# A megakernel's first part ordered anew: durations of the steps as the trace has them, and the standard deviation as a step of its own

## The chip, the cores and the metric

The kernel runs on one core of a Trainium2 chip. The metric is the device time of one execution in microseconds. Before the change it is 3328.47 us, the median of 3 runs (3323.04 to 3329.41).

## The reference

Sixteen images and texts go through a tokenizer and two layers, each with an attention and a feed-forward stage, all with a width of D = 256 and float32. The changed code lies in the tokenizer, the window attention and the routing of the experts:

```
h = tokens(x)                                  # conv 2x2, softmax(Q K^T / 16) V, 441 rows
h = concat([h, txt], axis=1)                   # 569 rows for each image
h = h + window_attention(layernorm(h))         # shifted windows of 64 rows, 8 heads
h = h + experts(layernorm(h))                  # 8 experts, the best two of each row
h = h + phase_attention(layernorm(h))
h = h + lstm(layernorm(h))

def _layernorm(x, axis=-1, eps=1e-5):
    m = jnp.mean(x, axis=axis, keepdims=True)
    v = jnp.var(x, axis=axis, keepdims=True)
    return (x - m) / jnp.sqrt(v + eps)
```

## The kernel before, in words

The rows of two images make a pair p (0 to 7), and a pair is cut into nine chunks c of 128 rows, each two windows of 64. Everything up to the scatter of the rows to their experts is the first part (about 950 of 3332 us). Behind it lie the experts, the phase attention and the recurrent network.

The first part's instructions are written out by a planner that runs while the kernel is built. Each stream of work is a Python generator. It yields the engine and the duration of its next step ("PE", 0.25), then issues the instruction. `Order.run` holds, for each engine, the time at which it would be free. It takes, of all streams, the step that could start first (ties go to the lower rank, then to the older stream), adds its duration and goes on. So the order of the instructions on TensorE, VectorE, ScalarE and GpSimd is fixed at build time by these durations, and the chip's waits come on top. A duration has no other effect. "DVE+" and "POOL+" mark steps that are not laid side by side with each other. `first.fork` starts a new stream that goes on beside the one that forks it.

The streams are: `features` (the convolution), `projections` (`tq`, `tv`), two of `tokens` (scores `tsc` in line 611, transposes `tpt`, averages `tav` in line 639, the rows `h`), `norms` (statistics and normalized rows `wxn`), four of `windows`, `routing` (softmax over the experts, ranks, positions `at`) and, forked, `sent_rows` (the second norm) and `send` (for each chunk two scatters by an indirect DMA in line 927). A chunk's window work on TensorE goes: transposes `wtr` (line 724), queries and keys `wqk` (734), scores `wsc` (752), values `wv` (768) and gate (777), transposes of the probabilities `wpt` (807), averages `wav` (819), output `wob` (830). Between them lie copies on ScalarE and VectorE: `wxT` (728), the keys `KB` (708, on both engines), queries `wq` (743), scaled scores `wS` (758), maximum (782), values `VB` (790), subtraction on GpSimd (794), exponential (796), sum and normalization (799 to 803), `wPT` (812), `wAT` (826).

`norm` (lines 657 to 674) takes VectorE's statistics, then does on GpSimd in one step: variance plus epsilon (668), to the power -1/2 (669), and, for the window's norm, to the power 1/2 (671). That last one, the standard deviation, is kept in a spare column of the row tile and read by line 784, which scales the gate's logits. Then VectorE normalizes (673). The pair of mean and variance has one buffer for all windows.

SP, which issues most DMAs (stores `HD`, loads of the experts' rows `xs` and weights `w`, of the recurrent weights `W_hh` and `W_ih`), isn't under the planner. The framework orders it by its own rules.

Of the kernel before, what the change touches and what calls it, by code (L numbers as in the profile page):

```python
# [10 lines left out]
F32 = mybir.dt.float32  # L11
BF16 = mybir.dt.bfloat16
AF = mybir.ActivationFunctionType
ALU = mybir.AluOpType
# [3 lines left out]
D = 256  # L18
# [3 lines left out]
E = 8  # L22
# [275 lines left out]
def kernel(ctx: ExitStack, tc: tile.TileContext, a: dict, out: bass.AP):  # L298
    nc = tc.nc
# [33 lines left out]
    def place_of(name, slot):  # L333
        return ps.tile([128, 512], F32, name=name, tag=f"first{slot}", bufs=1)
# [18 lines left out]
    slot = route.tile([128, NP, 2, NC], F32, name="slot")  # L353
# [24 lines left out]
    first = Order()  # L378
# [13 lines left out]
    def rows_of(p, c):  # L392

        while len(made) >= ROWS:
            before = ("normed", *made[len(made) - ROWS])
            if before in first.events:
                break
            yield "at", before
        made.append((p, c))
        H[p, c] = hp.tile([128, D + E + 1], F32, name=f"h{p}_{c}", tag="h", bufs=ROWS)  # L400
        return H[p, c]
# [198 lines left out]
    def tokens(slot):  # L600

        last = NIMG - 384
        for n in range(slot, 7 * NP, 2):
            p, c = divmod(n, 7)
            for s in range(2):
                yield "at", ("values", 2 * p + s)
            sc = place_of(f"tsc{n}", 4 + slot)
            for m in range(2):
                yield "PE", 0.76, "64"
                for s in range(2):  # L610
                    nc.tensor.matmul(
                        sc[64 * s : 64 * s + 64, :NIMG], QT[s][:, m, 64 * c : 64 * c + 64],
                        fTs[2 * p + s][:, m, :], start=(m == 0), stop=(m == 1),
                    )
            top = wk.tile([128, 1], F32, name=f"ttop{n}", tag=f"ttop{slot}", bufs=1)
            yield "DVE", 0.61
            nc.vector.tensor_reduce(top, sc[:, :NIMG], AX.X, ALU.max, negate=True)
            P = wk.tile([128, NIMG], F32, name=f"tP{n}", tag=f"tP{slot}", bufs=1)
            share_ = wk.tile([128, 1], F32, name=f"tsum{n}", tag=f"tsum{slot}", bufs=1)
            yield "ACT", 0.85  # L620
            nc.scalar.activation(P, sc[:, :NIMG], AF.Exp, bias=top, accum_out=share_)
            pt = place_of(f"tpt{n}", 4 + slot).rearrange("p (t n) -> p t n", t=4)
            for t in range(4):
                m = min(128, NIMG - 128 * t)
                yield "PE", TURN
                nc.tensor.transpose(pt[:m, t, :], P[:, 128 * t : 128 * t + m], ident)
            yield "DVE", 0.17
            nc.vector.reciprocal(share_, share_)
            PT = wk.tile([128, 4, 128], F32, name=f"tPT{n}", tag=f"tPT{slot}", bufs=1)
            yield "ACT", 0.5  # L630
            nc.scalar.copy(PT[:, :3, :], pt[:, :3, :])
            yield "ACT", 0.28
            nc.scalar.copy(PT[:last, 3, :], pt[:last, 3, :])
            mm = place_of(f"tav{n}", 4 + slot)[:, :D]
            for t in range(4):
                m = min(128, NIMG - 128 * t)
                yield "PE", 0.44, "64"
                for s in range(2):
                    nc.tensor.matmul(
                        mm[64 * s : 64 * s + 64, :], PT[:m, t, 64 * s : 64 * s + 64],  # L640
                        TV[s][:m, t, :], start=(t == 0), stop=(t == 3),
                    )
            if c < 6:
                yield from rows_of(p, c)
                to = [(slice(0, 128), c)]
            else:
                yield "at", ("text", p)
                to = [(slice(lo + 64 * s, hi + 64 * s), i) for s in range(2)
                      for lo, hi, i in ((0, 25, 6), (32, 64, 8))]
            for q, i in to:  # L650
                yield "DVE", 0.48
                nc.vector.scalar_tensor_tensor(
                    H[p, i][q, :D], mm[q], share_[q], tok_b[q], ALU.mult, ALU.add
                )
            first.mark(("token", p, c))

    def norm(h, to, name, slot):

        st = wk.tile([128, 6], F32, name=f"{name}_st", tag=f"st{slot}", bufs=1)
        yield "DVE", 0.43  # L660
        nc.vector.bn_stats(st, h[:, :D])
        mv = wk.tile([128, 2], F32, name=f"{name}_mv", tag=f"mv{slot}", bufs=1)
        yield "DVE", 0.18
        nc.vector.bn_aggr(mv, st)
        rstd = wk.tile([128, 1], F32, name=f"{name}_rstd", tag=f"rstd{slot}", bufs=1)
        yield "POOL", 0.85 if name[0] == "r" else 1.28
        over = mv[:, 1:2]
        nc.gpsimd.tensor_scalar(over, over, EPS, None, ALU.add)
        nc.gpsimd.tensor_tensor(rstd, over, mhalf[:, :1], ALU.pow)
        if name[0] == "w":  # L670
            nc.gpsimd.tensor_tensor(h[:, D + E :], over, half, ALU.pow)
        yield "DVE+", 0.5
        nc.vector.tensor_scalar(to, h[:, :D], mv[:, 0:1], rstd, ALU.subtract, ALU.mult)
        return rstd

    def norms():

        for n in range(NC * NP):
            p, c = unit(n)
            if n >= XNS:  # L680
                yield "at", ("turned", *unit(n - XNS))
            yield "at", ("token", p, min(c, 6)) if c != 7 else ("text", p)
            xn = xns[p, c] = wk.tile([128, D], F32, name=f"wxn{p}_{c}", tag="wxn", bufs=XNS)
            yield from norm(H[p, c], xn, f"w{p}_{c}", "w")
            first.mark(("columns", p, c))

    def sent_rows(p, c, h, slot):

        if p not in XN:
            if p > 1:  # L690
                yield "at", ("sent", p - 2)
            if p not in XN:
                LG[p] = wk.tile([128, NC, E], F32, name=f"LG{p}", tag="LG", bufs=2)
                XN[p] = xnp.tile([128, NC, WIDE], F32, name=f"XN{p}", tag="XN", bufs=2)
                yield "POOL", 0.2
                nc.gpsimd.tensor_copy(XN[p][:, :, D], cols[:, COL["row"] + NC * p : COL["row"] + NC * (p + 1)])
        rstd = yield from norm(h, XN[p][:, c, :D], f"r{p}_{c}", slot)
        yield "DVE", 0.19
        nc.vector.scalar_tensor_tensor(
            LG[p][:, c, :], h[:, D : D + E], rstd, frow("gate_b", E), ALU.mult, ALU.add  # L700
        )
        first.mark(("normed", p, c))

    def half_of_keys(u, kb, qk, rows, engine):
        for r in rows:
            own = slice(32 * r, 32 * r + 32)
            yield engine, 0.4
            (nc.scalar.copy if engine == "ACT" else nc.vector.tensor_copy)(
                kb[own, :, :, r, :], qk[own, 1].rearrange("p m (w x) -> p m w x", w=2)
            )  # L710
        first.mark(("keys", u, engine))

    def windows(slot):

        kb, vb = KB[slot], VB[slot]
        for n in range(slot, NC * NP, WINDOWS):
# [3 lines left out]
            h, xn = H[p, c], xns.pop((p, c))  # L720
# [9 lines left out]
            for m in range(2):  # L730
                for j in range(2):
                    for k in range(2):
                        yield "PE", 0.25
                        nc.tensor.matmul(  # L734
                            qk[:, j, m, :], wqkv[:, k, D * j + 128 * m : D * j + 128 * m + 128],
                            xT[:, k, :], start=(k == 0), stop=(k == 1),
                        )
# [33 lines left out]
                            start=(k == 0), stop=(k == 1),  # L771
                        )
            for k in range(2):
                yield "PE", 0.06, "64"
                for w in range(2):
                    own = slice(64 * w, 64 * w + 64)
                    nc.tensor.matmul(
                        vg[own, D : D + E], xT[:, k, own], gw[:, k, :], start=(k == 0), stop=(k == 1)
                    )
            top = wk.tile([128, NH], F32, name=f"wtop{u}", tag=f"wtop{slot}", bufs=1)  # L780
            yield "DVE", 0.68
            nc.vector.tensor_reduce(top, S, AX.X, ALU.max)
            yield "DVE", 0.2
            nc.vector.scalar_tensor_tensor(
                h[:, D : D + E], vg[:, D : D + E], h[:, D + E :], win_b[:, D:], ALU.mult, ALU.add
            )
            for odd in range(2):
                own = slice(64 * odd, 64 * odd + 64)
                yield "ACT", 0.4
                nc.scalar.copy(  # L790
                    vb[own, :, :, odd, :], v[own].rearrange("p w (g d) -> p w g d", g=4)
                )
# [144 lines left out]
    with tc.manual_schedule(engines=ENGINES):  # L937
# [9 lines left out]
        half = hp.tile([128, 1], F32, name="half")  # L947
# [9 lines left out]
        wk = first_part.enter_context(tc.tile_pool(name="first", bufs=1))  # L957
# [1012 lines left out]
    with tc.manual_schedule(engines=ENGINES):  # L1970
# [5 lines left out]
        wk = bg.enter_context(tc.tile_pool(name="pha", bufs=1))  # L1976
# [170 lines left out]
```

## Time and profile before

| | us |
|---|---|
| median of three runs | 3328.47 |
| profiled execution | 3333.89 |
| its span | 3332.1 |
| TensorE busy in the span | 3026.1 (91%) |
| VectorE / ScalarE / GpSimd busy | 2057.1 / 1448.2 / 821.3 |
| first part: last scatter's end | 954.2 |
| first matmul of the experts | 970.19 |

A profile shows one execution. Busy time is that of an engine's own instructions; the granted clock is the share of full speed that TensorE was allowed. A wait is idle time of an engine before an instruction, put down to what ended it. For an order that is fixed beforehand the waits of the bounding engine, TensorE, are what matters, stretch by stretch.

### The profile page before, as it was taken

What the parts mean: (1) busy time and instruction counts of PE and PEld (TensorE: products, weight loads), DVE (VectorE), ACT (ScalarE), POOL (GpSimd) and SP (SyncE); (2) the same over time, 40 slices, a digit from 0 to 9 for tenths busy, and PEclk for the clock granted to TensorE, in tenths of its full rate; (3) what the DMA queues carried; (4) which work ended last, traced back from release to release, by engine and by line L of the source; (5) the groups of instructions that cost most, each with busy time, mean ns of one, the idle gap of its engine ahead of it and who ended that gap; (6) DMA issues with size and microseconds to landing.
All of it is one profiled execution on the core that took longest, in us unless ns stands there. A gap on an engine that the chain in (4) does not pass through costs nothing.

```text
span 3332.1 us, 134813 instructions
## 1 busy us (share of the span) xinstructions
PE 3026.1 (91%) x57670; PEld 2213.9 (66%) x57670; DVE 2057.1 (62%) x6956; ACT 1448.2 (43%) x4986; POOL 821.3 (25%) x1581
## 2 busy tenths in 40 slices
PE   6999998999859999997999999999999999999884
PEld 3666666666648888885566666766666666666652
DVE  4777777776742322222676777767777777776555
ACT  3544544454312222222454555555555555454442
POOL 1354465445533322222311011011001011000000
PEclk9999999999969999998999999999999999999997
DMA  5111222101167676763334333332333232333333
GB/s 177 57 66 54 71 84 68 46 31 45 41 225 255 237 255 236 251 243 117 114 83 98 86 89 85 78 98 77 95 77 94 78 92 75 86 89 75 93 99 114
DMA packets 275481, 369.73 MB, mean 111 GB/s; under 512 B 144496, under 2 KB 219296, under 8 KB 262208
## 3 DMA queue, kind: packets, MB, share of 16 engines
q1 hardware_dynamic: 249104, 304.71, 30.6%
q0 software_dynamic: 14160, 38.83, 3.1%
q10 hardware_dynamic: 11616, 17.56, 1.8%
q8 instruction: 452, 7.41, 0.9%
q14 instruction: 149, 1.22, 0.1%
HBM read 243.13 MB, written 117.84 MB: 108 GB/s over the span
## 4 chain that ended last, share of the span: by engine, by line
PE 38%; DVE 7%; ACT 5%; issue 2%; DMA 1%; SPq 1%; POOL 0%; ACTq 0%; DVEq 0%; POOLq 0%
PE gates L1811 13%; PE xm_False L1105 5%; PE out_gate L1820 2%; PE z L1105 2%; PE ek L1105 2%; PE v L1105 2%; PE po_False L1105 2%; PE ds_False L1105 2%; PE eq L1105 1%; PE r_False L1105 1%; ACT act L1832 1%; ACT th L1868 1%; DVE ab L1847 1%; DVE cT L1860 1%; DVE act L1853 1%
## 5 line engine op out<-in xcount | busy, mean ns | idle before, releaser
L1811 PEld LDWEIGHTS gates<-W_hh,X 128*16 128x16 f32 (+1 forms) x18176 | 373.2, 103 | 260.3 <-DVE X L1875 246.3
L1811 PE MATMUL gates<-W_hh,X 128*16 128x96 f32 (+1 forms) x18176 | 487.8, 248 | 63.7 <-DVE X L1875 60.9
L1832 ACT ACTIVATE act<-gates 128x96 f32<-128x96 f32 x568 | 142.1, 250 | 446.0 <-PE gates L1811 438.5
L1316 ACT ACTIVATE hT<-hp,w 128x256 f32<-128x256 f32 (+1 forms) x332 | 132.9, 453 | 450.2 <-PE hp L1309 343.4
L1105 PE MATMUL xm_False<-W_ih,dxT_False 128*32 128x256 f32 x4352 | 291.8, 380 | 2.7 <-DVE dxT_False L1341 1.9
L1847 DVE SCALAR_TENSOR_TENSOR ab<-act 128x64 f32<-128x64 f32 x568 | 128.1, 226 | 258.3 <-ACT act L1832 250.8
L1323 PE MATMUL y<-w,hT 128*128 128x256 f32 x1208 | 276.3, 381 | 6.9 <-ACT hT L1316 6.5
L1309 PE MATMUL hp<-xt,w 128*128 128x256 f32 (+1 forms) x1328 | 277.7, 362 | 0.0
L1329 DVE TENSOR_TENSOR ys<-y,w 128x512 f32<-128x512 f32 (+1 forms) x83 | 53.4, 643 | 360.6 <-PE y L1323 315.8
L1754 PEld LDWEIGHTS <-nil 128*32 128x32 bf16 x4552 | 189.5, 94 | 112.7 <-issue 53.7
L1309 PEld LDWEIGHTS hp<-xt,w 128*128 128x128 f32 x1328 | 234.8, 192 | 29.3
L1323 PEld LDWEIGHTS y<-w,hT 128*128 128x128 f32 x1208 | 226.3, 190 | 41.7 <-ACT hT L1316 11.2
L1250 POOL DMA_INDIRECT YT<-ys,to x151 | 147.7, 978 | 416.4 <-DVE ys L1329 389.3
L1820 PE MATMUL out_gate<-W_hh,X 128*32 128x64 f32 x9088 | 232.5, 220 | 1.6 <-issue 1.6
L1760 ACT COPY gates<-xc 128x96 f32<-128x96 f32 x569 | 138.6, 244 | 182.6 <-DMA xc<-XCD 75.5
L1820 PEld LDWEIGHTS out_gate<-W_hh,X 128*32 128x32 f32 x9088 | 186.6, 110 | 4.5 <-issue 1.8
L1875 DVE SCALAR_TENSOR_TENSOR X<-toT,th 128x32 f32<-128x32 f32 x569 | 110.0, 193 | 122.0 <-ACT th L1868 117.4
L1371 POOL TENSOR_SCALAR d_False_rstd<-d_False_mv 128x2 f32<-128x2 f32 (+1 forms) x36 | 9.2, 256 | 673.2 <-DVE d_False_mv L1363 514.9
L1868 ACT ACTIVATE th<-cT 128x32 f32<-128x32 f32 x569 | 130.5, 229 | 94.2 <-DVE cT L1860 43.0
L927 POOL DMA_INDIRECT XS<-XN,at x144 | 149.9, 1041 | 51.6 <-issue 24.9
L734 PE MATMUL wqk<-wxT,wqkv 128*128 128x128 f32 x1152 | 150.9, 280 | 9.6 <-ACT wxT L728 9.2
L734 PEld LDWEIGHTS wqk<-wxT,wqkv 128*128 128x128 f32 x1152 | 140.5, 193 | 25.7 <-ACT wxT L728 16.0
(384 smaller groups left out, 6556.1 us busy)
## 6 DMA issues: line engine op xcount, KB each, us to landing
w<-in_wpack SPq DMA_DIRECT2D x83, 1154.0 KB
taps<-in_taps SPq DMA_DIRECT2D x16, 1764.0 KB
xc<-XCD SPq DMA_DIRECT2D x71, 384.0 KB
XCD<-xp_False SPq DMA_DIRECT2D x256, 96.0 KB
yg<-YT SPq DMA_DIRECT2D x72, 256.0 KB
xs<-XS SPq DMA_DIRECT2D x68, 258.0 KB
HD<-h SPq DMA_DIRECT2D x72, 128.0 KB
fh<-HD SPq DMA_DIRECT2D x72, 128.0 KB
```

The costliest lines, as they stand in the source:

```text
L734: nc.tensor.matmul(qk[:, j, m, :], wqkv[:, k, D * j + 128 * m : D * j + 128 * m + 128], xT[:, k, :], start=(k == 0), stop=(k == 1),)
L927: fill(0, nc.gpsimd.indirect_dma_start(out=XS[0], out_offset=bass.IndirectOffsetOnAxis(ap=at[:, i, c - lo : c - lo + 1], axis=0), in_=XN[p ...
L1105: nc.tensor.matmul(out[own], lhsT[:, own], rhs, start=start, stop=stop)
L1250: keep(nc.gpsimd.indirect_dma_start(out=YT, out_offset=bass.IndirectOffsetOnAxis(ap=to[:, i : i + 1], axis=0), in_=ys[:, i, :], in_offset= ...
L1309: nc.tensor.matmul(hp[:, i, : 128 * n], w1[:, k, hc * 128 : (hc + 1) * 128], xT[:, k, :], start=(k == 0), stop=(k == 1),)
L1323: nc.tensor.matmul(y[:, i, :], hT[:, hc, 128 * i : 128 * i + 128], w2[:, hc, :], start=(hc == 0), stop=(hc == 3),)
L1754: nc.tensor.matmul(g[32 * q : 32 * q + 32, :n], nil[:, :32], nil[:, :n], start=True, stop=last)
L1811: nc.tensor.matmul(GC[32 * q : 32 * q + NB * (1 + half), :96], before[:, kk, NB * (1 - half) :], Whh[:, kk, own : own + 96], start=False, ...
L1820: nc.tensor.matmul(GO[32 * q : 32 * q + 32, :64], before[:, kk, :], Whh[:, kk, own : own + 64], start=False, stop=(kk == 1),)
L1832: nc.scalar.activation(act[:, :96], GC[:, :96], AF.Tanh, scale=0.5), begun.pop((k, t))
L1847: nc.vector.scalar_tensor_tensor(ab, act[:, :64].rearrange("p (g x) -> p g x", g=2), 1.0, act[:, 64:].rearrange("p (g x) -> p g x", g=2), ...
L1868: nc.scalar.activation(th.rearrange("p k x -> p (k x)"), cT, AF.Tanh, scale=0.5)
```

## The change

Eleven durations of the first part get other values: matmul steps (0.76 to 0.745, 0.44 to 0.46, 0.25 to 0.225, 0.06 to 0.087), the normalization on VectorE (0.5 to 0.46), the two small scalings (0.19 to 0.25, 0.2 to 0.22), the key copies (0.4 to 0.46 on ScalarE and 0.53 on VectorE), the value copies (0.4 to 0.47) and GpSimd's step in the norm (0.85 or 1.28 to 0.9). The standard deviation leaves that step: `deviation` is forked as a stream of its own with 0.6 us on GpSimd. Mean and variance of the window's norm get three buffers. What is computed stays the same.

```diff
-                yield "PE", 0.76, "64"
+                yield "PE", 0.745, "64"
...
-                yield "PE", 0.44, "64"
+                yield "PE", 0.46, "64"
...
-        mv = wk.tile([128, 2], F32, name=f"{name}_mv", tag=f"mv{slot}", bufs=1)
+        mv = wk.tile([128, 2], F32, name=f"{name}_mv", tag=f"mv{slot}", bufs=3 if slot == "w" else 1)
...
-        yield "POOL", 0.85 if name[0] == "r" else 1.28
+        yield "POOL", 0.9
...
         if name[0] == "w":
-            nc.gpsimd.tensor_tensor(h[:, D + E :], over, half, ALU.pow)
-        yield "DVE+", 0.5
+            first.fork(deviation(h, over))
+        yield "DVE+", 0.46
         nc.vector.tensor_scalar(to, h[:, :D], mv[:, 0:1], rstd, ALU.subtract, ALU.mult)
         return rstd
+
+    def deviation(h, over):
+        yield "POOL", 0.6
+        nc.gpsimd.tensor_tensor(h[:, D + E :], over, half, ALU.pow)
...
-        yield "DVE", 0.19
+        yield "DVE", 0.25
...
-            yield engine, 0.4
+            yield engine, 0.46 if engine == "ACT" else 0.53
...
-                        yield "PE", 0.25
+                        yield "PE", 0.225
...
-                yield "PE", 0.06, "64"
+                yield "PE", 0.087, "64"
...
-            yield "DVE", 0.2
+            yield "DVE", 0.22
...
-                yield "ACT", 0.4
+                yield "ACT", 0.47
```

## The prediction

> **What bounds the kernel now.** The change touches only the first part, so I cut the span into stretches first. Columns: stretch and length in us, then busy time and instruction count of PE, PEld, DVE, ACT, POOL, then granted clock, DMA share, GB/s.
>
> ```profile
> 100.00:200.00 100.00, 96.11 (x871) 67.28 (x868) 77.24 (x207) 48.83 (x132) 34.85 (x64) 1.00 0.15 52
> 500.00:600.00 100.00, 89.03 (x780) 62.98 (x778) 71.14 (x196) 46.22 (x127) 53.32 (x93) 0.97 0.21 73
> 900.00:950.00 50.00, 27.00 (x206) 20.84 (x206) 32.84 (x137) 13.02 (x34) 25.95 (x45) 0.66 0.26 83
> 950.00:1000.00 50.00, 27.60 (x118) 23.80 (x119) 15.18 (x64) 8.39 (x22) 8.05 (x16) 0.69 0.87 302
> 1000.00:1050.00 50.00, 49.57 (x249) 43.57 (x248) 12.65 (x46) 10.49 (x26) 13.97 (x26) 1.00 0.76 260
> ```
>
> TensorE bounds the body: from 100 to 900 it is idle 60.7 of 800 us. From 900 to 970 no engine is full; a chain of small steps runs (the tail). From 975 on TensorE is full again, now with the experts. Second, PE's waits in the body (us, times, longest); the first four lines are links inside a window:
>
> ```profile
> PE wav L819 <- ACT wPT L812: 8.5, 14, 1.0
> PE wpt L807 <- DVE wS L803: 6.9, 11, 1.2
> PE wqk L734 <- ACT wxT L728: 6.5, 12, 1.2
> PE wv L768 <- DVE wS L758: 6.1, 14, 0.8
> PE tv L586 <- ACT tV L592: 6.0, 7, 2.9
> PE tq L567 <- ACT fT L549: 5.7, 1, 5.7
> ```
>
> All waits of this view sum to about 65 us, in pieces under 1 us mostly. That is all that a better order of the body can win.
>
> Third, the tail and what follows, from the timeline (start, us, engine):
>
> ```profile
> 929.46 1.05 POOL L794 TENSOR_TENSOR wS<-wS,wtop 128x512 f32<-128x512 f32 x1
> 943.46 0.43 SPq L1032 DMA_DIRECT2D W_hh<-in_W_hh  x1
> 961.49 0.88 SPq L1230 DMA_DIRECT2D w<-in_wpack  x2
> 970.19 2.79 PE L1279 MATMUL xtr<-ident,xs 128*128 128x128 f32 x12 [23.23 <-DMA xs<-XS]
> 973.95 0.46 SPq L1033 DMA_DIRECT2D W_ih<-in_W_ih  x1
> ```
>
> The last window's subtraction on POOL comes at 929.46, 4.5 us after its maximum was ready, because five scatters stand before it. The last window's output product ends at 939.2, the last scatter at 954.2, and PE starts the experts at 970.19 after 23 us without work.
>
> **What the edits change, part by part.** No instruction is added or removed. Comparing the built programs, PE, ACT, DVE and POOL have the same order from the last routing block on, so I carry 970 to 3332 over unchanged except for its start. Before that the order differs on every engine, and SP's differs until the sixth expert load.
>
> *The standard deviation apart.* The groups (mean ns):
>
> ```profile
> L669 POOL TENSOR_TENSOR w_rstd<-w_mv,mhalf 128x1 f32<-128x1 f32 x72 | 43.3, 602 | 6.0
> L671 POOL TENSOR_TENSOR h<-w_mv,half 128x1 f32<-128x1 f32 x72 | 42.5, 591 | 0.0
> L708 DVE COPY KB<-wqk 32x256 f32<-32x256 f32 x144 | 61.3, 426 | 70.7 <-ACT KB L708 27.4 <-ACT wq L743 24.7 <-PE wqk L734 8.1
> L790 ACT COPY VB<-wv 64x256 f32<-64x256 f32 x144 | 52.3, 366 | 135.1 <-DVE h L784 116.6 <-DVE ahead L885 7.2 <-DVE wtop L782 4.1
> ```
>
> POOL still does 72 x (0.26 + 0.60 + 0.59) us. The normalization already waits on the chip for the first power only, so no wait goes away there; the plan only stops placing it 0.38 us late. If a scatter (1.27 us) now stands before the second power, what waits is line 784, which comes after a matmul, a scaling and a maximum (over 2 us later): nothing. Three buffers for mean and variance free the next window's statistics from the second power: 0 to -0.5 us, taken as 0. Without that cover each late power would cost up to 1.27 us.
>
> *The durations.* Per window the plan gains on DVE 2 x 0.13 (key copies) + 0.06 + 0.02 - 2 x 0.04 = +0.26 us, on ACT 2 x 0.06 + 2 x 0.07 = +0.26, and on PE it loses 8 x 0.025 - 2 x 0.027 = 0.15. The start-to-start times agree: two key copies on ACT follow each other no closer than 0.37 us where other copies of that size take 0.27. So the old plan held the feeders some 0.4 us per window too early against PE, of 12.0 us that a window takes (866 us / 72). I count its price in two steps.
>
> (a) *Cover.* On PE's order of both programs I wrote each step's start-to-start time from the timeline (weights-times-window product 0.224 per matmul, score 0.37, token values 0.23, output 0.55, transposes 0.12, ...) and summed the PE work between a producer and its consumer. Where it is below what lies between them (transposed window copied: 0.75 us; probabilities copied: 1.0; keys 2.4; scores to values 1.0; softmax 5.0; average copied 0.75), PE must wait. Shortfall, before to after: window turned to products 9.6 to 5.1; keys 2.6 to 0.7; probabilities 9.0 to 8.6; softmax 7.5 to 2.8; scores 1.5 to 1.7; average 2.9 to 3.9; the token and projection links 12.7 to 13.6. Split by place: body 27.3 to 25.0 us, tail 18.4 to 11.4. The body's 27.3 is less than half of the 65 that the waits show: cover alone does not explain them. Body: -2.3.
>
> (b) *Queues.* The other 65 - 27 = 38 us are waits with enough cover on PE, where DVE or ACT was late in its own queue. These are what wrong durations cause. If each of some 60 such waits (mean 0.6 us) lost its whole 0.4 us it would be -24; if the greedy choice only trades them for others, 0. I take a quarter of the 24, -6, since most of the 95 waits are shorter than 1 us and a new order makes new ones; ends 0 and -14.
>
> *The tail.* After the last token product the old order has 40.0 us to the last window's scores (start 917.95), 10.6 of it idle. The new order leaves 1.7 us less PE work there and has 5 to 6 us more cover: about 33. The new order puts the last subtraction ahead of the scatters (-5 us), but the routing of the last tokens behind it: by the DVE and POOL rows, scores to output product 18.2 us (21.3 before), then 8.5 us to the positions of three column blocks, six scatters at 1.27, then the last block's four: last scatter at +38.2 after the scores, where it was +36.3. With the 1.7 us of PE work that moved ahead, the tail gives -7 + 1.7 + 1.9 = -3.4; half of it is sure enough to take: -2.
>
> *The load that moved.* On SP the 1 MB load of W_ih now stands right behind W_hh, before the first expert loads, not after the sixth row load. DMA is full from 944 to 960 (share 0.91 to 1.11, 220 to 415 GB/s in stretches of 2 us), and the first expert load waits for the scatters (SP's wait on them: 9.2 us). At 415 GB/s 1 MB is +2.5 us, at 300 +3.5. If the scatters did not share with SP's transfers it would be 0. The Trainium skill speaks against the change here ("DMA: Bandwidth & Descriptors", section "Issuing engines are not separate DMA queues": transfers from the scalar, sync and gpsimd engines run on the same 16 DMA engines and interleave). By the rule +2.5, by separate queues 0; the full share in the row sides with the rule: +2.5. It gives nothing back at 974, where PE waits for no weights after 975. The four smaller loads that now stand before the sixth weights (1.1 MB) wait at a buffer anyway (14.0 us in SP's waits): 0.
>
> *The clock.* The tail runs at 0.50 from 920 to 980 and does 12 us of PE work before 940; at full clock it would be 6. The skill's page "TensorE: Matmul & The Clock Gate" (section "HAM oscillation") asks for no idle gap above some 3.4 us. By that rule a denser tail would stay fast: -6. But here the clock fell with gaps of 2.3 us at most before it (905.01, 921.25). The new tail has gaps of that size too, so I take 0.
>
> Sum: -2.3 - 6 - 2 + 2.5 = -7.8 us. The profiled execution took 3333.89 (span 3332.1, 1.8 around it), 5.4 above the median of 3328.47. On its scale 3326; on the median's 3320.7.
>
> **The rivals.** *No change that shows*: the greedy order trades waits, (b) is 0, tail and load cancel: -2 us, 3326. For it: the number of changes between PE's tile shapes is 176 in both orders, and probabilities are as short as before. Against it: the shortfall falls by 45% where the window is turned and by 60% at the softmax, the two links with the longest feeders.
>
> *A larger gain*: (b) -14, the tail -3.4 with the last subtraction's 5 us: -17 or more, 3309. For it: the plan's errors all lean one way. Against it: 60.7 us is all the idle time.
>
> *Slower: the late routing.* All of the last pair's routing now stands behind the last subtraction, so 18 scatters (23 us) follow each other at the end. From the last output product to the last scatter I get 21.2 us, where it was 15.0: +6.2, and W_ih +3.5 behind it. It decides if the last output product does not come more than about 5 us earlier: with (b) at 0, +9.7 - 2.3 = +7.4, 3336.
>
> **How the numbers follow.** 0.2% is 6.7 us, about what a measurement of this kernel can tell from no change (its three runs spread over 6.4). Forecast (-5 to -13): 0.42; larger gain (-13 and more): 0.2; no change (-5 to +4): 0.2; slower (+4 and more): 0.18. Faster by over 0.2%: four fifths of the forecast's stretch and all of the larger gain, 0.54. Slower by over 0.2%: five sixths of the slow case, 0.15. The rest is 0.31. Range: 3304 (larger gain, with W_ih's load hidden and half of the subtraction's 5 us more) to 3336 (the slow case's value), which leaves out a quarter of each of those two; the forecast's own is 3315 to 3324.
>
> **What would show it.** Right: PE's waits in the body fall from 65 to 55-59 us, mainly at lines 724-734 and 803-807; the last subtraction follows its maximum within 1 us; W_ih is issued before 945 relative to the old clock and PE's wait for the first rows stays 20-27 us; from the experts on every line as before. Wrong if the body's waits stay at 65 or their kind only changes, if the last scatter ends over 15 us after the last output product by more than the tail gained, or if the later stretch changes length.

## The result, and the profile after

The changed kernel takes 3316.59 us, the median of 11 runs (3308.43 to 3319.79). The kernel before takes 3324.12 beside it (11 runs, 3319.81 to 3329.41). The ratio is 0.9978, with a 95% interval of 0.9970 to 0.9986. That is 7.5 us less, where 7.8 less was forecast. The ratio lies just outside the 0.2% that I called no change, though the interval reaches inside it. The total came out almost as forecast, but mostly from other places than the working named.

The same five stretches as before, for the changed kernel: stretch, length, busy time and count of PE, PEld, DVE, ACT, POOL, then granted clock, DMA share and GB/s. This is its profiled execution (3319.79 us, span 3318.0).

```profile
100.00:200.00 100.00, 96.70 (x879) 66.83 (x877) 76.95 (x209) 49.22 (x134) 34.48 (x64) 1.00 0.15 52
500.00:600.00 100.00, 93.83 (x861) 69.34 (x861) 76.63 (x209) 51.24 (x140) 55.37 (x98) 0.98 0.21 75
900.00:950.00 50.00, 16.84 (x96) 11.87 (x96) 28.94 (x142) 6.43 (x19) 23.29 (x43) 0.51 0.54 165
950.00:1000.00 50.00, 40.05 (x185) 34.71 (x186) 9.93 (x36) 9.08 (x22) 8.57 (x16) 0.84 0.83 295
1000.00:1050.00 50.00, 49.35 (x247) 43.31 (x247) 12.90 (x51) 11.35 (x29) 13.93 (x26) 1.00 0.67 232
```

The body is a little denser from 500 to 600 (93.83 against 89.03); over the seven hundreds from 100 to 800 it is 657.7 us of work against 650.5. The large change is in the fourth row: 40.05 us of TensorE work instead of 27.60, because the experts begin earlier. Their first transposes start at 958.49, not at 970.19.

PE's waits in the body (34 to 875) sum to 57.5 us in 75 waits, where it was 64.4 us in 97: fewer waits, and longer ones. The copied window, for one, has 9 waits of up to 2.5 us, where it had 12 of up to 1.2. (Lines are 4 later than before from the fork on.)

The tail, from the timeline (start, us, engine):

```profile
908.22 1.04 POOL L798 TENSOR_TENSOR wS<-wS,wtop 128x512 f32<-128x512 f32 x1
914.93 1.09 POOL L931 DMA_INDIRECT XS<-XN,at  x1 [5.67 <-DVE LG L703]
918.11 2.13 PE L834 MATMUL wob<-wout,wAT 128*128 128x264 f32 x4 [0.53 <-ACT wAT L830]
927.17 0.74 SPq L1037 DMA_DIRECT2D W_ih<-in_W_ih  x1
938.75 0.96 POOL L931 DMA_INDIRECT XS<-XN,at  x1 [0.19 <-issue]
958.49 2.79 PE L1283 MATMUL xtr<-ident,xs 128*128 128x128 f32 x12 [27.34 <-DMA xs<-XS]
```

The last subtraction (908.22) now stands ahead of the scatters, whose last run begins at 914.93. The last output product ends at 920.2 (it was 939.2), the last scatter at 939.7 (954.2). So the window chain gained 19 us and the scatters 14.5: a part of the gain is given back to the routing, which now comes after the last output product.

One execution of each is a thin base: this execution's body was short (the last token product ends at 868.5 us; in the five other executions of this TensorE order it ends at 873.7 to 876.7, and their waits sum to 59.3 to 60.2 us). So both unchanged kernels were run once more side by side, below, and the account is made on that pair.

### The profile page after: what moved, and what is told of

It is laid out like the page before. It is cut to its first block, busy times and chain, and to the rows that moved or that the text cites. A ratio compares the mean times of both kernels' runs of the same rounds, so it can differ in the third digit from the quotient of the medians.

```text
span 3318.0 us, 134767 instructions
## 1 busy us (share of the span) xinstructions
PE 3024.1 (91%) x57670; PEld 2218.2 (67%) x57670; DVE 2051.1 (62%) x6956; ACT 1449.8 (44%) x4986; POOL 817.8 (25%) x1581
## 4 chain that ended last, share of the span: by engine, by line
PE 39%; DVE 7%; ACT 4%; issue 2%; DMA 1%; SPq 1%; POOL 0%; ACTq 0%; DVEq 0%; POOLq 0%
PE gates L1815 13%; PE xm_False L1109 6%; PE out_gate L1824 3%; PE ek L1109 2%; PE po_False L1109 2%; PE z L1109 2%; PE v L1109 2%; PE ds_False L1109 2%; PE eq L1109 1%; PE r_False L1109 1%; ACT act L1836 1%; ACT th L1872 1%; DVE ab L1851 1%; DVE cT L1864 1%; DVE act L1857 1%
## 5 line engine op out<-in xcount | busy, mean ns | idle before, releaser
L738 PEld LDWEIGHTS wqk<-wxT,wqkv 128*128 128x128 f32 x1152 | 141.5, 194 | 26.5 <-ACT wxT L732 11.8
```

Of the source, the lines that this page charges most:

```text
L738: nc.tensor.matmul(qk[:, j, m, :], wqkv[:, k, D * j + 128 * m : D * j + 128 * m + 128], xT[:, k, :], start=(k == 0), stop=(k == 1),)
```

## The experiments

All ratios are against the kernel before, run beside it on the same chip. There are three series, each on another chip, where the kernel before took 3339.55, 3335.88 and 3323.49 us in the median. So medians of different series are not compared (a stretch of a trace is, where the series has none of its own).

### Which part of the change carries it

*Durations alone.* The changed kernel with the standard deviation back inside the norm's step (1.5 us as one piece) and with one buffer:

```diff
-        mv = wk.tile([128, 2], F32, ..., bufs=3 if slot == "w" else 1)
+        mv = wk.tile([128, 2], F32, ..., bufs=1)
-        yield "POOL", 0.9
+        yield "POOL", 0.9 if name[0] == "r" else 1.5
-            first.fork(deviation(h, over))
+            nc.gpsimd.tensor_tensor(h[:, D + E :], over, half, ALU.pow)
```

> The new durations, with the second power left inside the norm's step (1.5 us planned there for the window's norm, as the rows say) and one buffer. If the right durations carry the gain (theory: plan fits chip, so PE waits less in the body), the body's end (last token product, 878.1 before, 868.5 changed) comes at 866 to 872 and the time is 3314 to 3320. If the fork carries it (rival), 3324. If any new order is a draw of the greedy choice (rival: luck), anything from 3312 to 3330.

Measured: 3350.02 us, ratio 1.0031 (1.0019 to 1.0043), slower than before. Idle time of PE from 34 us to the last token product grows to 76.1 us (66.2 before). Its PE waits (34 to 875):

```profile
PE wtr L728 <- DVE wxn L673: 9.3, 8, 2.6
PE wqk L738 <- ACT wxT L732: 8.5, 15, 0.9
PE tq L567 <- ACT tQ L576: 7.4, 4, 3.5
```

The wait for the normalized window (line 673) leads here; it is among the leading waits neither before nor after the change. The tail keeps the old form: 62.3 us from the last token product to the last output product, 15.0 from there to the last scatter (61.2 and 15.0 before).

*The fork alone.* The kernel before with `deviation` as its own stream and three buffers, all other durations old:

```diff
-        yield "POOL", 0.85 if name[0] == "r" else 1.28
+        yield "POOL", 0.85
-            nc.gpsimd.tensor_tensor(h[:, D + E :], over, half, ALU.pow)
+            first.fork(deviation(h, over))
+    def deviation(h, over):
+        yield "POOL", 0.43
+        nc.gpsimd.tensor_tensor(h[:, D + E :], over, half, ALU.pow)
```

> The kernel before with the second power as a step of its own (0.43 us planned there, 0.85 for the rest) and three buffers; all other durations old. By the theory that durations carry the gain: the body as before within 3 us, 3321 to 3327. By the rival that the fork carries it: 3317. By luck: anything from 3312 to 3330.

Measured: 3337.13 us, ratio 0.9997 (0.9989 to 1.0004). Its tail has the new form, 51.7 us to the last output product and then 20.9 to the last scatter, a gain of 3.6 against the first trace of the kernel before, but of 1.2 against its second (below); the body's idle time is 67.1. Neither part alone brings what both bring. Each of them reorders the part anew. The programs have 4016 matmuls ahead of the experts; at 2599 of these places another kind of matmul stands with the fork alone than before, and at 3075 with durations alone than with the full change.

### The load of W_ih and the gap before the experts

*W_ih late.* The changed kernel with one line different; the order on TensorE is that of the changed kernel:

```diff
-        nc.sync.dma_start(Wih, kxn("W_ih"))
+        nc.scalar.dma_start(Wih, kxn("W_ih"))
```

> The changed kernel with its order on PE, DVE, ACT and POOL kept, but W_ih's 1 MB is issued from ScalarE's queue after the second expert tile and so lies behind the scatters. If SP's transfers and the scatters share the DMA engines (the step of the prediction that costs the moved load +2.5 us), the time from the last scatter's issue (ends 939.7 in the changed kernel) to the experts' first transpose (958.5) falls from 18.8 us to about 16, and the run is 2 to 3.5 us faster than the changed kernel: about 3314. If they don't share (rival: a hidden load), the gap stays at 18.8 and the time at 3316.6.

*All recurrent loads late.* The same for the two loads of `lstm_b` and for `W_hh`:

```diff
-            nc.sync.dma_start(t, a["lstm_b"][of].to_broadcast([128, 4 * D]))
-        nc.sync.dma_start(Whh, kxn("W_hh"))
-        nc.sync.dma_start(Wih, kxn("W_ih"))
+            nc.scalar.dma_start(t, a["lstm_b"][of].to_broadcast([128, 4 * D]))
+        nc.scalar.dma_start(Whh, kxn("W_hh"))
+        nc.scalar.dma_start(Wih, kxn("W_ih"))
```

> As the run before, with both bias rows (512 KB each) and W_hh (1 MB) also behind the scatters on ScalarE's queue: 3 MB less before the experts. By the shared engines at 300 to 415 GB/s the gap from last scatter to first transpose falls by 7 to 10 us until something else ends it (the zero fills of 2 MB and the loading of the plan's registers), so I expect 13 us or less and 3309 to 3312. By the rival (own queues) no change: 3316.6. ScalarE spends 2 us on four more issues among the first expert tiles, which may show as a wait of PE of up to 2 us there.

Measured: 3325.11 us, 0.9957 (0.9943 to 0.9970), and 3326.02 us, 0.9966 (0.9952 to 0.9979). Both look better than the change's own 0.9978, but that was measured on another chip. In the second the framework filled the free place on SP with other loads, so it doesn't say what the gap is without traffic: from 927.64 on, `Wk`, `Wq`, `Wv`, `Wo` and four more stand there, ahead of the last scatter. Hence a second series with the unchanged kernels in it.

*Both unchanged kernels again*, the kernel before and the changed kernel, with no edit:

> The kernel before, unchanged, for its trace on the same chip as the next three. Stage times as in its first profile (last token product 878, last output product 939, last scatter 954, first transpose 970) or all of the body later by some us, as the runs of the first experiments had it. From last scatter to first transpose: 16.0 us if that gap is the program's, about 18 if it is the chip's.

> The changed kernel, unchanged, beside the others. Ratio 0.9978 as before. If the moved load costs anything, the gap from last scatter to first transpose is 2 to 3 us longer than that of the kernel before in this same call; if the gap of 18.8 was the chip's, they are within 1 us.

*W_ih late again*, the same kernel as above:

> As the first experiment, now beside the changed kernel itself. If the moved load costs 2.5 us: ratio lower than the changed kernel's by 0.0007 and the gap shorter by 2 to 3 us. If it is hidden: the same within 0.0004 and the gap the same within 1 us. The first experiment's ratio, 0.9957, would be 0.0021 lower than the changed kernel's in another call, more than the load can give.

*All thirteen loads late.* Every load of that block (4.7 MB) goes to ScalarE's queue, spread behind the experts' tiles 1 to 8, so that none of them stands in the gap:

```diff
-        nc.sync.dma_start(Whh, kxn("W_hh"))
-        nc.sync.dma_start(Wih, kxn("W_ih"))
+        yield "at", ("tile", 0, 2)
+        nc.scalar.dma_start(Whh, kxn("W_hh"))
+        yield "at", ("tile", 0, 3)
+        nc.scalar.dma_start(Wih, kxn("W_ih"))
...
```

> The changed kernel with all thirteen weight and bias loads of the later parts (4.7 MB) issued from ScalarE's queue behind the first eight expert tiles, a few at a time. If the DMA engines' traffic sets the gap: from last scatter to first transpose 12 to 14 us, ratio 0.996 or lower. If the zero fills, the scatters' own landing and the small steps behind them set it: within 1 us of the changed kernel's gap and the ratio the same.

Measured side by side (the last four columns are us in the profiled executions, where a product counts by its end; the gap is from the last scatter's end to the first transpose, the experts from the first to the last of their transposes):

| kernel | ratio (interval) | last token product to last output product | last output product to last scatter | gap | experts |
|---|---|---|---|---|---|
| before | 0.9997 (0.9990 to 1.0004) | 58.8 | 15.0 | 18.7 | 547.7 |
| changed | 0.9976 (0.9967 to 0.9985) | 48.6 | 19.8 | 20.3 | 545.3 |
| W_ih late | 0.9977 (0.9969 to 0.9984) | 48.6 | 19.9 | 19.4 | 545.9 |
| all loads late | 0.9974 (0.9965 to 0.9983) | 48.5 | 20.5 | 16.6 | 547.7 |

The W_ih kernel had 0.9957 in the first series and has 0.9977 here, equal to the changed kernel beside it. So ratios of different series can differ by about 0.2%, as much as is looked for, and the better ratio of the first says nothing of W_ih. With W_ih gone the gap is 0.8 us shorter and the experts 0.6 longer: no cost shows in the total. With all 4.7 MB gone the gap is 3.6 us shorter, but the experts take 2.4 more and the time is the same. These gaps are of one execution each, and the gap of one and the same kernel varies: 16.0 and 18.7 us in the two traces of the kernel before, 18.8 and 20.3 in those of the changed kernel. So 0.8 us is within that spread. The 3.6 point to the transfers without proving their size.

The pair before and changed gives the account. First, TensorE up to the last token product and from there to the last output product (columns as above), kernel before, then changed kernel:

```profile
34.00:875.18 841.18, 776.70 (x6967) 544.06 (x6966) 619.45 (x1676) 401.40 (x1095) 411.44 (x723) 0.99 0.18 62
875.18:933.97 58.79, 40.12 (x356) 30.96 (x356) 41.33 (x134) 20.09 (x51) 38.59 (x69) 0.83 0.16 55
34.00:875.08 841.08, 779.76 (x6963) 549.71 (x6962) 615.75 (x1676) 405.00 (x1101) 410.37 (x721) 0.98 0.18 62
875.08:923.73 48.65, 36.04 (x359) 26.45 (x358) 38.31 (x116) 17.79 (x45) 30.48 (x55) 0.92 0.13 45
```

The last token product ends at 875.2 and 875.1 us. That alone doesn't make the two bodies equally fast, since the new order has more of the windows' work ahead of it. Behind it stand 64 of the products for queries and keys before the change and 48 after:

```profile
L734 PE MATMUL wqk<-wxT,wqkv 128*128 128x128 f32 x64 | 9.4, 305 | 2.7 <-ACT wxT L728 2.7
L738 PE MATMUL wqk<-wxT,wqkv 128*128 128x128 f32 x48 | 6.5, 281 | 1.6 <-ACT wxT L732 1.6
```

With fewer transposes and more of the short value products behind it, 1.7 us of TensorE's work moved ahead by the prediction's own count. PE's idle time in the body falls from 64.5 to 61.3 us. Its waits there (34 to 875), kernel before:

```profile
PE wav L819 <- ACT wPT L812: 8.8, 16, 1.0
PE wpt L807 <- DVE wS L803: 6.2, 10, 1.2
PE wqk L734 <- ACT wxT L728: 6.2, 12, 1.2
```

and changed kernel:

```profile
PE wv L772 <- DVE wS L762: 6.5, 8, 2.4
PE tq L567 <- ACT tQ L576: 5.7, 5, 1.9
PE wqk L738 <- ACT wxT L732: 5.2, 9, 2.5
PE wpt L811 <- DVE wS L807: 5.1, 5, 1.7
PE wav L823 <- ACT wPT L816: 3.1, 6, 1.0
```

The sum falls only from 62.7 to 60.2 us. The wait for the copied probabilities falls by 5.7; longer waits for `tQ` (576, by 3.4) and others take most of it back. So on equal work the body is about 2 us faster (1.7 and the 0.1 of its end). The idle time fell by more, 3.2 us, but TensorE was also busy for 3.1 us more: 1.7 with the moved work, and the other 1.4 by my estimate because the granted clock was 0.98 there instead of 0.99.

Second, the start of the experts from the timeline, kernel before:

```profile
967.61 2.79 PE L1279 MATMUL xtr<-ident,xs 128*128 128x128 f32 x12 [25.90 <-DMA xs<-XS]
972.77 1.12 PE L1279 MATMUL xtr<-ident,xs 128*128 128x128 f32 x4 [2.37 <-DMA xs<-XS]
973.68 9.12 PE L1309 MATMUL hp<-xt,w 128*128 128x256 f32 x30
```

the changed kernel:

```profile
963.83 2.80 PE L1283 MATMUL xtr<-ident,xs 128*128 128x128 f32 x12 [29.04 <-DMA xs<-XS]
967.97 1.11 PE L1283 MATMUL xtr<-ident,xs 128*128 128x128 f32 x4 [1.35 <-DMA xs<-XS]
968.88 7.67 PE L1313 MATMUL hp<-xt,w 128*128 128x256 f32 x30
```

and the kernel with all loads late:

```profile
960.44 2.93 PE L1291 MATMUL xtr<-ident,xs 128*128 128x128 f32 x12 [26.08 <-DMA xs<-XS]
966.26 1.12 PE L1291 MATMUL xtr<-ident,xs 128*128 128x128 f32 x4 [2.90 <-DMA xs<-XS]
967.17 8.44 PE L1321 MATMUL hp<-xt,w 128*128 128x256 f32 x30
```

The first transposes start 3.4 us earlier with all loads late than in the changed kernel, the first expert's products only 1.7: PE waits longer for the next rows (2.90 instead of 1.35). Then those thirty products take 8.44 us instead of 7.67. The clock explains the second part. These are the products alone (line of `hp`; stretch, length, busy time and count of PE and PEld, granted clock, DMA share, GB/s), before, changed, all loads late:

```profile
973.60:978.60 5.00, 4.92 (x12) 4.01 (x13) 0.50 1.01 398
978.60:982.60 4.00, 4.00 (x19) 3.34 (x18) 0.99 0.72 277
968.80:970.90 2.10, 2.02 (x5) 1.74 (x6) 0.50 1.02 391
970.90:976.40 5.50, 5.50 (x26) 4.50 (x25) 1.00 1.03 369
967.10:970.90 3.80, 3.73 (x9) 3.08 (x10) 0.51 1.00 403
970.90:975.40 4.50, 4.50 (x22) 3.76 (x20) 1.00 0.11 40
```

A product takes about 0.41 us at a granted clock of 0.50 and 0.21 at full clock. The clock rises 11.0 us after the first transpose before the change and 7.1 after it. With all loads late it rises 10.4 us after: the experts start 3.4 us earlier than in the changed kernel, but the clock comes back at the same moment, 970.9. Of the 3.4 us, 1.6 go into the longer wait and 0.8 into products at half clock; the last of the experts' transposes ends 0.9 us earlier.

### Is the order a draw?

If true durations are what helps, a change of a few ns in two of them should leave the gain, and old durations changed by as little should stay slow or become no better. If the greedy choice is a draw, any of these may land anywhere. All four move the token softmax's two durations (lines 616 and 620 of the changed kernel) or take back PE's durations:

```diff
-            yield "DVE", 0.61
+            yield "DVE", 0.607
-            yield "ACT", 0.85
+            yield "ACT", 0.848
```

> The changed kernel with two of its planned durations 2 and 3 ns shorter (a token's exponential 0.848, its maximum 0.607): as true to the chip as before, but about half of PE's instructions of the first part stand in another order. Theory 'true durations': as the changed kernel, ratio 0.9977 within 0.001. Theory 'any order is a draw': the cover that was counted on PE's order of the changed kernel (36.3 us short, the kernel before 45.7) decides; here it is 48.3 us short, so 2.6 us over the kernel before: ratio 1.0008, 1.000 to 1.002.

The same two lines with 10 ns less (0.600 and 0.840):

> The changed kernel with the same two durations 10 ns shorter. 'True durations': 0.9977. 'A draw', by cover: 33.9 us short, 11.8 less than the kernel before: ratio 0.9965. In the order, the routing of the last pair's middle blocks stands ahead of the last output product, so from that product to the last scatter 15 us, not 19.8.

The changed kernel with PE's four durations old:

```diff
-                yield "PE", 0.745, "64"
+                yield "PE", 0.76, "64"
...
-                yield "PE", 0.46, "64"
+                yield "PE", 0.44, "64"
...
-                        yield "PE", 0.225
+                        yield "PE", 0.25
...
-                yield "PE", 0.087, "64"
+                yield "PE", 0.06, "64"
```

> The changed kernel with PE's four durations as they were before; those of VectorE, ScalarE and GpSimd new. 'True durations': loses part of the gain, 0.998 to 0.9995. 'A draw', by cover: 33.7 us short, 12 less than the kernel before: 0.9964. Last output product to last scatter 15 us, as in the run before.

The kernel before with the 10 ns less in the same two lines:

> The kernel before with the same two durations 10 ns shorter and nothing else. 'True durations': as the kernel before, within 0.0008. 'A draw', by cover: 43.0 us short, 2.7 less: 0.9992; the tail has 4.7 us more cover but the late routing of the changed kernel (+4.8 us), so nearer 1.000.

Measured side by side, where the kernel before took 3323.49 us (times in us; "cover" is the difference to before that step (a)'s count on PE's order gives for body and tail together):

| kernel | median | ratio (interval) | first transpose | cover |
|---|---|---|---|---|
| changed, 2 to 3 ns less | 3338.80 | 1.0044 (1.0030 to 1.0058) | 972.5 | +2.6 |
| changed, 10 ns less | 3316.14 | 0.9977 (0.9967 to 0.9987) | 953.2 | -11.8 |
| changed, PE's durations old | 3323.92 | 1.0000 (0.9991 to 1.0008) | 961.1 | -12.0 |
| before, 10 ns less | 3336.59 | 1.0037 (1.0023 to 1.0050) | 972.6 | -2.7 |

Two or three ns in two durations that the change doesn't touch put another kind of matmul at 2021 of the 4016 places and make the changed kernel slower than before by 0.44%. Over the four the time spans 22.7 us, three times the change's gain, and the first transpose 19.4: nearly all of it arises ahead of the experts. Part of what the slowest lost lies between the last token product and the last output product. There it and the kernel with 10 ns less have the same matmuls to do (columns as above, slowest first):

```profile
879.96:941.10 61.14, 39.59 (x306) 30.42 (x306) 41.53 (x124) 15.86 (x40) 46.02 (x81) 0.72 0.20 70
870.43:919.93 49.50, 33.56 (x307) 25.69 (x306) 37.82 (x122) 15.62 (x40) 27.57 (x48) 0.83 0.12 40
```

Of the 11.6 us between them 5.6 are idle time of TensorE (21.5 against 15.9), and 6.0 are the same work at a lower clock (granted 0.72 against 0.83). The waits have other reasons as well. From 868 to 960, slowest:

```profile
PE pos L897 <- DVE ahead L892: 11.9, 2, 6.5
PE wpt L811 <- DVE slot L915: 4.4, 1, 4.4
PE wpt L811 <- DVE r_mv L664: 3.6, 1, 3.6
```

The last two are transposes of the probabilities held up by VectorE's work for the routing and for the second norm, which that order put in front of the windows' steps. The kernel with 10 ns less, same stretch, has neither; there the transposes wait for the probabilities themselves:

```profile
PE wpt L811 <- DVE wS L807: 9.9, 2, 7.4
PE pos L897 <- DVE ahead L892: 8.3, 2, 6.8
```

It also needs only 15.1 us from the last output product to the last scatter, since it keeps the routing of the last pair's middle blocks ahead of that product. So the change's late routing isn't a price of true durations either; it goes with the draw. The count of cover ranks these orders roughly (its two largest gains are the two quickest), but misses the size by 12 to 16 us for all except the second.

## Why the prediction was right or wrong

The total and the side came out, and the gain does come from a better order of the first part, but the working behind them was mostly wrong. By the pair of traces in the second series (spans 3335.4 and 3328.6, so -6.8 in all) the terms are:

| term | forecast | measured |
|---|---|---|
| body, (a) and (b) | -8.3 | -0.1 by its end, -1.8 on equal work |
| tail, last token product to last scatter | -2 | -10.1 + 4.9 = -5.3, or -3.6 on equal work |
| W_ih and gap | +2.5 | +1.6 |
| experts | 0 | -2.4 |
| rest behind them | 0 | -0.6 |

"On equal work" books the 1.7 us of moved work where it stood before the change, as the forecast of the tail did. It is one pair: the rest behind the experts, where nothing was changed, took 1814 to 1821 us in the fourteen traces, so 0.6 is no finding.

*The standard deviation as its own step, 0.* Its instructions stayed (72 of 0.58 us on GpSimd, no one waits for them). That the move costs nothing is not separately shown: the fork alone gave 0.9997, but with an order of its own.

*Step (a), cover in the body, -2.3: about right.* PE's waits fell by 2.5 in the pair. The link by link count wasn't right, though: it left the probabilities' link at 9.0 to 8.6, and that is the one whose wait fell most (8.8 to 3.1).

*Step (b), queues, -6: this step failed.* It held that the remaining waits come from durations that are false by some 0.4 us per window, and that true ones would take away a quarter of them. The waits in the body fell by 2.5 us, hardly more than (a)'s share; they became fewer and longer. (In the changed kernel's first trace they fell by 6.9, in none of the five other traces of its order by more than 5.1.) The runs with 2 to 10 ns changed contradict the idea behind the step: with durations as true as the change's, the time is 0.44% above before or 0.23% below, and PE's old durations bring it back to 1.0000. What the runs show in its place is that the order decides, and that it turns on which of many near ties the greedy choice falls on. The rival that put (b) at 0 had that part right. Its total of -2 was too small, since it kept the tail and the load as forecast and put nothing on the experts.

*The tail, -2: right mechanism, mis-sized.* The parts that I worked out were last token product to last scores 40.0 to 33, scores to output product 21.3 to 18.2, and output product to last scatter 15.0 to 21.2. In the pair they are 37.6 to 32.4, 21.2 to 16.2, and 15.0 to 19.8. So the way to the scores won 5.1 us, not 7, and the way from there to the last scatter cost nothing (36.2 to 36.1), where my parts give +3.1. The late routing, the mechanism of the slower rival, is there with +4.9 of its 6.2; the earlier output product pays for it. My sum also had a slip: 18.2 + 8.5 + ten scatters of 1.27 is 39.4, not 38.2, so that the parts give -2.2 and not -3.4. The halving to -2 hid this. (The range has such a slip too: its lower end follows from its parts as 3306, not 3304.) The last subtraction does stand ahead of the scatters, but 1.9 us after its maximum, not within 1: in the changed kernel's first trace GpSimd does a second norm's two steps in between (907.38 and 907.68). Before the change it came 5.2 us after (924.27 to 929.46), not 4.5.

*W_ih, +2.5: failed.* It was issued early, as forecast (927.17 in the lines above, right behind `W_hh`). Taking it away changes the time by nothing that shows (0.9977 against 0.9976), though the gap was 1.6 us longer in the pair. The Trainium skill's rule, "DMA: Bandwidth & Descriptors", section "Issuing engines are not separate DMA queues", isn't contradicted: with all 4.7 MB away the gap was shorter by 3.6 us, or 0.8 us for each MB. My price was three times that, because I let the whole megabyte's transfer stand on the path. In the changed kernel's second trace SP waits in the gap for other things too before the first row loads: 2.3 us for a small VectorE step (line 1202) and 4.4 us for the zero fill of the rows. Nor did I follow the price to the end: the experts gave 2.4 us of the shorter gap back, since neither the next rows nor the clock came as much earlier as the first transpose did.

*From the experts on as before: this step failed, by 2.4 us.* They are shorter by about that in both pairs of traces (547.5 to 545.3, and 547.7 to 545.3). In the lines above all of it lies in the first expert's start: the wait for its next rows falls from 2.37 to 1.35, and the first thirty products from 9.12 to 7.67, since they run at half clock for a shorter time. The other traces agree. In the four in which the clock rises 10.4 us or more after the first transpose the experts take 547.5 to 547.7 us, in the ten others 545.3 to 546.7. Carrying that stretch over unchanged left out that it starts at half clock.

*The clock, 0: right ahead of the experts, not behind.* From 930 until the experts start the granted clock is 0.50 in both kernels of the pair. The denser tail did not stay fast, so the -6 that the Trainium skill's rule would have allowed ("TensorE: Matmul & The Clock Gate", section "HAM oscillation") did not come. From 34 us to the first transpose TensorE is busy for 817.9 us in both. Behind it the shorter time at half clock is worth 1.4 us, as said.

The errors cancelled, which is luck: on equal work 6.5 us too much in the body, against 1.6 too little in the tail, 0.9 too dear in the gap, and 3.0 overlooked behind it. Two of the signs of being wrong that I had named came true: the waits mainly changed their kind, and the later stretch changed its length.

Open: whether true durations are better than false ones on average. Four orders of one kind and four of the other, on up to three chips each, show no difference: with the changed kernel's PE durations the ratios are 0.9976, 1.0044, 0.9977 and 1.0031, with the old ones 1.0000, 0.9997, 1.0037 and 1, so the means are 1.0007 and 1.0009. But with this spread a difference of 0.2% would not be seen. And no order here is clearly better than the changed kernel: that with 10 ns less (0.9977) and that with all loads late (0.9974) lie within its interval.

## What to carry to other kernels

An order made by a greedy planner is one draw: before a gain is put down to better durations, change some durations by a few ns and measure the spread, here 23 us between four such orders against a gain of 7.5. Then measure several draws and keep the best, looking first at the tail (what still stands between the last product of the bounding engine and the next stage), since here the body, busy for 92% of its time, won only some 2 us. When two orders are cut at the same instruction, count the work on each side first. Where tenths of a per cent are compared, run the unchanged kernels beside every variant. And follow a freed gap to the end of the next stage before counting it: here a longer wait and the half clock took most of it back.

## What the runs showed of the hardware that was not expected

Small dependent steps on VectorE stood apart with nothing to wait for but the step before. From the timeline of the kernel with all recurrent loads late:

```profile
936.66 0.19 DVE L1167 TENSOR_REDUCE expert<-past 128x4 f32<-128x32 f32 x1
937.86 0.17 DVE L1168 TENSOR_SCALAR where<-expert 128x4 int32<-128x4 f32 x1 [1.02 <-DVE expert L1167]
939.29 0.18 DVE L1172 TENSOR_REDUCE first<-past 128x4 f32<-128x32 f32 x1 [1.17 <-DVE past L1169]
941.41 0.17 DVE L1174 TENSOR_SCALAR first<-first 128x4 f32<-128x4 f32 x1 [1.25 <-issue]
```

and the same steps in the changed kernel's first trace:

```profile
933.97 0.19 DVE L1167 TENSOR_REDUCE expert<-past 128x4 f32<-128x32 f32 x1
934.19 0.23 DVE L1168 TENSOR_SCALAR where<-expert 128x4 int32<-128x4 f32 x1
934.49 0.19 DVE L1172 TENSOR_REDUCE first<-past 128x4 f32<-128x32 f32 x1
```

From the first of them to the last step of this series it takes 7.8 us in eight of the traces and 9.7 to 12.6 in six, and the changed kernel has 7.8 in one execution and 11.2 in another. The load on DMA doesn't separate them: from 925 to 945 its share is 0.89 in the first trace above and 0.97 in the second. What it costs in total wasn't measured, and its cause is open. The changed kernel's trace with 11.2 us is the one of the pair, so some of its longer gap may come from this and not from W_ih.
